# Down product of a mixture of experts with seven half-size products in place of eight

## The chip, the cores and the metric

The kernel runs on one core of one Trainium2 chip. All arithmetic shown here is in 32-bit floating point. The metric is the device time of one execution in microseconds; before the change it is 651.7 us, the median of three runs (650.91 to 652.51).

## The reference, cut to what matters

Two layers are added to the input x of 2048 tokens by 512. The first picks one of four gated feed-forward matrices by token number. The second normalises, chooses 4 of 32 experts per token by a gate, and adds a shared expert:

```
logits = x @ gate_w.T;  topk_w, topk_ids = top_k(softmax(logits), 4)      # weights normalised to 1
gu = einsum('ech,ehf->ecf', buf, w13)          # buf: the tokens of an expert, 512 wide
g, u = split(gu, 2)                            # 256 each
act = silu(g) * u
eo = einsum('eci,eih->ech', act, w2)           # the down product: 256 -> 512
routed.at[token].add(eo * weight)
out = residual + routed + shared
```

What the change touches is the line with w2, the down product of an expert, and the weighting after it.

## The kernel before, in words

The first part of the kernel (to about 270 us) does the first layer, the gate and the shared expert, and scatters the normalised rows into a table in DRAM, one section per expert. The experts are then ordered by how many tokens they have: *rank* 0 is the fullest. The loop over the 32 ranks (L1132) is unrolled and does, per rank r:

- issue the loads for later ranks on SyncE's queue: the rows of rank r+3 (`fetch`), both weight matrices of rank r+5 (`weights`, L882), each as soon as its tile is free;
- turn the rows of rank r+1 on VectorE (a transpose of 128x1024 at L944) and scale them (L950, L954);
- `up_rank` (L1013): 16 products of 128x128 weights by up to 256 tokens, silu on ScalarE, two multiplications on VectorE that make `aT`, the activations with the inner dimension on the partitions;
- `given` and `tokens_of`: the weights and token numbers of the rows;
- `down_rank` (L1033): for each half of 128 tokens two accumulating products 128x128 by 512 columns into one bank of PSUM (`po`), which ScalarE multiplies by the tokens' weights (`weighted`, L987) into a tile `eo`;
- `push` (L992): an indirect DMA on GpSimd's queue that adds the 128 rows to the output in DRAM. Additions of one rank may overlap; those of different ranks follow each other, since they can hit the same rows.

Ranks up to 17 can hold more than 256 tokens. Their surplus goes through six *blocks* that pack the rests of two or four ranks into 128 rows (`up_block`, `turn_block_act`, `down_block` L1069, and one more `push` per rank, `out<-eo_x`). The widths of ranks 26 and up are 240 and 228 tokens, all others 256:

```
LOW = ((26, 240), (29, 228))
```

The tiles that matter: `eo` has four buffers, `po` two banks, the up products three banks and a share of two more, `aT` two buffers, w2 six. The program is written in the order above; the framework places the instructions on each engine's queue by their readiness in its own plan, so that products of rank r+1 can stand between those of rank r, and sets the waits. The hint `behind` fixes the order of two instructions on one engine.

Of the kernel before, what the change touches and what calls it, by code (L numbers as in the profile page):

```python
# [8 lines left out]
F32 = mybir.dt.float32  # L9
# [3 lines left out]
ALU = mybir.AluOpType  # L13
# [4 lines left out]
P = 128  # L18
T = 2048
D = 512  # L20
# [9 lines left out]
CM = 256  # L30
MJ = CM // P
I = 256
IC = I // P
# [3 lines left out]
NB = 4  # L37
# [9 lines left out]
RW = D + 2 * K + 1  # L47
# [12 lines left out]
def tile_xattn_moe(  # L60
# [15 lines left out]
    nc = tc.nc  # L76

    const = ctx.enter_context(tc.tile_pool(name="const", bufs=1))
# [5 lines left out]
    ps_o = ctx.enter_context(tc.tile_pool(name="ps_o", bufs=2, space=PSUM))  # L84
# [6 lines left out]
    ctx_pool = first.enter_context(tc.tile_pool(name="ctx", bufs=1))  # L91
# [19 lines left out]
    shw13 = keep.tile([P, DC, 2 * I], F32, name="shw13")  # L111
    shw2 = keep.tile([P, IC, D], F32, name="shw2")

    none = const.tile([P, NB, RW], F32, name="none")

    def second_inputs(after_):

# [80 lines left out]
    def behind(ins, other, kind=mybir.DependencyClass.NoSync):  # L198

        tc.add_manual_dep(  # L200
            ins.ins,
            other.ins.name,
            mybir.DependencyInfo(kind, mybir.DependencyReason.DATA),
            reason="order",
        )
# [21 lines left out]
    n = EX * NT  # L227
# [73 lines left out]
    xw = ctx_pool.tile([P, XB], F32, name="xw")  # L301
# [502 lines left out]
        return er, er_x, er_i, over_i  # L804


    muls_s, adds_s = [], []

    def glu_up(xT, w13t, name):
# [131 lines left out]
    def turn_parts(z, name, after_=None):  # L941
        n = z.shape[1] * SQ
        xT = late.tile([P, DC, n], F32, tag=f"xT{n}", name=f"xT_{name}", bufs=2)
        ins = nc.vector.transpose(  # L944
            xT.rearrange("p c (r b) -> p r c b", b=SQ), z.rearrange("p r (a c) -> p r c a", c=DC)
        )
        if after_ is not None:
            behind(ins, after_)
        h = 2 if n > P else DC
        ins = nc.vector.tensor_tensor(  # L950
            xT[:, :h, :], xT[:, :h, :], nwq[:, :h].unsqueeze(2).to_broadcast([P, h, n]), ALU.mult
        )
        for c in range(h, DC):
            nc.scalar.mul(xT[:, c, :], xT[:, c, :], nwq[:, c : c + 1])  # L954
        return xT, ins
# [31 lines left out]
    def weighted(po, wt, name, tag, m=P):  # L987
        eo = last.tile([P, D], F32, tag=tag, name=f"eo_{name}", bufs=4 if tag == "eo" else 2)
        nc.scalar.mul(eo[:m, :], po[:m, :], wt[:m, :])  # L989
        return eo  # L990

    def push(eo, dst, group=None):  # L992

        put = nc.gpsimd.indirect_dma_start(  # L994
            out=out,
            out_offset=bass.IndirectOffsetOnAxis(ap=dst, axis=0),
            in_=eo,
            in_offset=None,
            bounds_check=T - 1,
            oob_is_err=False,  # L1000
            compute_op=ALU.add,
        )
        if group is not None:
            if group in adds:
                tc.declare_no_dep(put.ins, group=group, reason="of one expert: other rows")
            tc.add_to_no_dep_group(group, put.ins)
            adds[group] = put

    def width(r):

        return min([CM] + [n for r_, n in LOW if r >= r_])

    def up_rank(xT, w13t, n, name, after_):  # L1013

        pg = ps_m.tile([P, IC, CM], F32, tag="mm", name="pg")
        pu = [
            ps_m.tile([P, CM], F32, tag="mm", name="pu"),
            ps_t.tile([P, CM], F32, tag="tp", name="pu"),
        ]
        for ps, f in [(pg[:, f, :n], f) for f in range(IC)] + [(pu[f][:, :n], IC + f) for f in range(IC)]:  # L1020
            for c in range(DC):
                last_up = nc.tensor.matmul(  # L1022
                    ps, w13t[:, c, f * P : (f + 1) * P], xT[:, c, :n], start=(c == 0), stop=(c == DC - 1)
                )
        s = last.tile([P, IC, CM], F32, tag="silu", name="s", bufs=2)
        nc.scalar.activation(s[:, :, :n], pg[:, :, :n], AF.Silu)  # L1026
        aT = last.tile([P, IC, CM], F32, tag="aTm", name=f"aT_{name}", bufs=2)
        for f in range(IC):
            ins = nc.vector.tensor_tensor(aT[:, f, :n], s[:, f, :n], pu[f][:, :n], ALU.mult)  # L1029
            behind(ins, after_)  # L1030
        return aT, ins, last_up

    def down_rank(aT, w2t, wt, to, n, r):  # L1033
        for j in range(MJ):
            m = min(P, n - j * P)
            po = ps_o.tile([P, D], F32, tag="po", name="po")
            for f in range(IC):
                nc.tensor.matmul(  # L1038
                    po[:m, :], aT[:, f, j * P : j * P + m], w2t[:, f, :], start=(f == 0), stop=(f == IC - 1)
                )  # L1040
            eo = weighted(po, wt[:, j : j + 1], f"{r}_{j}", "eo", m)
            push(eo[:m, :], to[:m, j : j + 1], f"rank{r}")
# [23 lines left out]
        nc.vector.tensor_copy(aT, tp)  # L1066
        return aT

    def down_block(aT, ws):  # L1069
        m = P // len(ws)  # L1070
        po = ps_o.tile([P, D], F32, tag="po", name="po")
        for f in range(IC):
            for i, (_, w2t) in enumerate(ws):
                rr = slice(i * m, (i + 1) * m)
                nc.tensor.matmul(po[rr, :], aT[:, f, rr], w2t[:, f, :], start=(f == 0), stop=(f == IC - 1))
        return po


# [28 lines left out]
    wt = [weights(0), weights(1)]  # L1107
# [6 lines left out]
    last = ctx.enter_context(tc.tile_pool(name="last", bufs=1))  # L1114
# [17 lines left out]
    for r in range(E):  # L1132
        if r + AHEAD < E:
            got[r + AHEAD] = fetch(r + AHEAD)
        if r + AHEAD in before:
            rows_x[r + AHEAD] = block_in(r + AHEAD)
        for q in ahead[r]:
            if q < E:
                wt.append(weights(q))
        if r == E - 1:  # L1140
            need = nc.values_load(over_i[0:1, 0:1], min_val=0, max_val=E)
        if r + 1 < E:
            xT_next, next_ = turn_parts(got[r + 1][0], f"{r + 1}")
        aT, made, last_up = up_rank(xT, wt[r][0], width(r), f"r{r}", next_)
        pend = block_up(r, turned_x, last_up) if r in before else None
        wr = given(got[r][1], er[:, r : r + 1], f"{r}", made)
        to = tokens_of(got[r][1][:, :, RW - D - 1], to_all[:, r, :], made)
        if r + 1 in before:
            turned_x = block_turned(r + 1, rows_x.pop(r + 1), made)
        down_rank(aT, wt[r][1], wr, to, width(r), r)  # L1150
        if pend:
            n, rs_, ws, a, xw, tox = pend
            aTx = turn_block_act(a, f"x{n}")
            eo = weighted(down_block(aTx, ws), xw[:, 0:1], f"x{n}", "eo_x")
            m = P // len(rs_)
            for i, q in enumerate(rs_):
                part[q] = eo[i * m : (i + 1) * m, :], tox[:m, i : i + 1]
        xT = xT_next
        if r in part:
            push(*part[r], f"rank{r}")  # L1160
# [3 lines left out]
    with tc.If(need > 0):  # L1164
# [57 lines left out]
        n = E * C // P  # L1222
# [94 lines left out]
```

## Time and profile before

| | |
|---|---|
| median of 3 runs | 651.7 us |
| the profiled execution's own time | 652.45 us |
| its span, first to last instruction | 650.6 us |
| PE busy | 621.1 us (95%) |
| DVE busy | 285.2 us (44%) |
| ACT busy | 174.7 us (27%) |
| POOL busy | 245.2 us (38%) |
| L1038 down products, 256 records | 116.5 us |
| L1022 up products, 1024 records | 117.7 + 114.0 us |
| L994 additions to the output, 82 | 100.5 + 24.7 us |

PE is the matrix engine, PEld its weight loads, DVE is VectorE, ACT ScalarE, POOL GpSimd, SP SyncE. A name such as `po<-w,aT_r` is the tile written and the tiles read; `x8` counts the records merged into one row. A bracket at the end of a row holds the engine's idle time before it and what ended it; a wait for several things is put down to the one that came last by the profile. Records of one engine can overlap in time, so the distance between starts tells the pace.

### The profile page before, as it was taken

The numbers are of one execution on the slowest core, as the hardware profiler recorded it, in microseconds if no ns is written. First come the engines' busy times: TensorE is split into PE (matmuls) and PEld (weight loads), VectorE is DVE, ScalarE is ACT, GpSimd is POOL, SyncE is SP. The second block draws the span as 40 slices with busy tenths as digits, with TensorE's granted clock in tenths as the row PEclk, the third lists the DMA queues.
The fourth block names the chain that finished last, engine by engine and source line by source line (L and its number), as shares of the span: only waits on it lengthen the run. The fifth ranks groups of instructions, "written<-read, shape, count | busy, mean of one in ns | idle before, by whom it ended". The sixth has DMA issues, their size and how long they took to land.

```text
span 650.6 us, 8462 instructions
## 1 busy us (share of the span) xinstructions
PE 621.1 (95%) x2396; PEld 375.3 (58%) x2396; DVE 285.2 (44%) x766; ACT 174.7 (27%) x311; POOL 245.2 (38%) x217
## 2 busy tenths in 40 slices
PE   5999999999996999999999999999999999999991
PEld 2454555555542444556557577567567777687780
DVE  7655556675733812633424344243243342424410
ACT  1223454454321000122222222222222223222220
POOL 4451002356573465432234333424332413233331
PEclk9999999999996999999999999999999999999997
DMA  7489990325272596799979979979999999998442
GB/s 260 132 316 422 417 418 34 129 88 213 101 268 110 168 398 200 197 313 177 273 170 250 283 146 291 299 162 275 287 270 272 262 245 267 236 260 126 60 51 35
DMA packets 90120, 144.42 MB, mean 222 GB/s; under 512 B 19152, under 2 KB 56016, under 8 KB 83408
## 3 DMA queue, kind: packets, MB, share of 16 engines
q1 hardware_dynamic: 72064, 101.53, 50.5%
q0 software_dynamic: 18000, 42.26, 27.1%
q8 instruction: 21, 0.34, 0.2%
q14 instruction: 35, 0.29, 0.1%
HBM read 79.05 MB, written 66.00 MB: 223 GB/s over the span
## 4 chain that ended last, share of the span: by engine, by line
PE 76%; DMA 7%; SPq 6%; issue 4%; DVE 2%; another core or an unknown queue 1%; POOL 1%; ACT 1%; DVEq 0%; POOLq 0%
PE po L1038 14%; PE pg L1022 14%; PE pu L1022 14%; PE po L461 10%; PE pp L440 9%; SPq L897 4%; PE pg L816 3%; DMA w<-in_w 3%; PE tp L429 2%; PE po L831 2%; PE pp_x L1051 2%; PE pu L816 2%; DMA out<-eo,to_all 2%; DMA z<-s_dram 2%
## 5 line engine op out<-in xcount | busy, mean ns | idle before, releaser
L994 POOL DMA_INDIRECT out<-eo,to_all x64 | 100.5, 1571 | 147.9 <-ACT eo L989 90.2
L1022 PE MATMUL pg<-xT,w 128*128 128x256 f32 (+2 forms) x512 | 117.7, 377 | 0.0
L1038 PE MATMUL po<-w,aT_r 128*128 128x512 f32 (+2 forms) x256 | 116.5, 595 | 0.1
L1022 PE MATMUL pu<-xT,w 128*128 128x256 f32 (+2 forms) x512 | 114.0, 376 | 0.0
L1022 PEld LDWEIGHTS pg<-xT,w 128*128 128x128 f32 x512 | 96.3, 190 | 27.2 <-issue 17.0
L1029 DVE TENSOR_TENSOR aT_r<-s,pu 128x256 f32<-128x256 f32 (+2 forms) x64 | 26.7, 417 | 186.7 <-PE pu L1022 169.7
L1022 PEld LDWEIGHTS pu<-xT,w 128*128 128x128 f32 x512 | 97.3, 190 | 11.5
L989 ACT ACTIVATE eo<-po,wt 128x512 f32<-128x512 f32 x64 | 44.0, 687 | 148.8 <-PE po L1038 147.8
L1038 PEld LDWEIGHTS po<-w,aT_r 128*128 128x128 f32 (+2 forms) x256 | 47.6, 188 | 51.5 <-issue 40.0
L614 POOL DMA_INDIRECT s_dram<-h,slot x64 | 62.2, 973 | 36.0 <-issue 16.3
L440 PE MATMUL pp<-cT,xT 128*128 (+1 forms) x152 | 72.1, 597 | 1.4 <-issue 0.6
L461 PE MATMUL po<-cT,aT 128*128 (+1 forms) x152 | 68.4, 592 | 0.0
L944 DVE STREAM_TRANSPOSE xT<-z 128x1024 f32<-128x1024 f32 x32 | 65.2, 2038 | 3.2 <-DMA z<-s_dram 2.8
L994 POOL DMA_INDIRECT out<-eo_x,to_x x18 | 24.7, 1371 | 89.9 <-DMA out<-eo,to_all 43.2
L461 PEld LDWEIGHTS po<-cT,aT 128*128 128x128 f32 x152 | 27.5, 190 | 27.7 <-issue 27.5
L440 PEld LDWEIGHTS pp<-cT,xT 128*128 128x128 f32 x152 | 26.7, 190 | 27.4 <-issue 24.3
L583 POOL TENSOR_TENSOR rs<-rs,mhalf 128x2 f32<-128x2 f32 x16 | 11.3, 704 | 78.8 <-DVE rs L582 78.8
L1026 ACT ACTIVATE s<-pg 128x512 f32<-128x512 f32 (+2 forms) x32 | 18.9, 590 | 71.2 <-PE pg L1022 65.1
L954 ACT ACTIVATE xT<-xT,nwq 128x256 f32<-128x256 f32 x64 | 28.7, 498 | 23.7 <-DVE xT L944 10.2
L831 PE MATMUL po<-shw,aT_s 128*128 128x512 f32 x64 | 32.5, 650 | 2.1 <-issue 1.8
L816 PE MATMUL pg<-h2T,shw 128*128 128x512 f32 x64 | 29.2, 596 | 0.0
L403 ACT ACTIVATE hn<-acc,rv 128x512 f32 (+1 forms) x19 | 15.2, 802 | 50.8 <-DVE rv L387 30.9
(186 smaller groups left out, 541.7 us busy)
## 6 DMA issues: line engine op xcount, KB each, us to landing
w<-in_w SPq DMA_DIRECT2D x32, 1024.0 KB
s_dram<-none SPq DMA_DIRECT2D x1, 20840.0 KB
w<-in_w SPq DMA_DIRECT2D x32, 512.0 KB
z<-s_dram SPq DMA_DIRECT2D x128, 128.0 KB
h_dram<-h SPq DMA_DIRECT2D x4, 1042.0 KB
cT<-in_ctxT SPq DMA_DIRECT2D x4, 1024.0 KB
out<-none SPq DMA_DIRECT2D x1, 1024.0 KB
s_dram<-h,slot POOLq DMA_INDIRECT x64
```

Of the source, the lines that this page charges most:

```text
L440: ins = nc.tensor.matmul(ups[b], xT_[b][:, c, :], cT[:, bass.ds(off[b], 1), c, :].rearrange("p o f -> p (o f)"), start=(c == 0), stop=(c = ...
L461: ins = nc.tensor.matmul(po, aT_[b][:, f, :], cT[:, bass.ds(off[b], 1), f, :].rearrange("p o f -> p (o f)"), start=(f == 0), stop=(f == DC ...
L614: put = nc.gpsimd.indirect_dma_start(out=table, out_offset=bass.IndirectOffsetOnAxis(ap=index, axis=0), in_=src, in_offset=None,)
L816: ins = nc.tensor.matmul(ps, w13t[:, c, fo * P : (fo + 1) * P], xT[:, c, :], start=(c == 0), stop=(c == DC - 1))
L831: ins = nc.tensor.matmul(po, aT[:, f, i * P : (i + 1) * P], w2t[:, f, :], start=(f == 0), stop=(f == IC - 1))
L944: ins = nc.vector.transpose(xT.rearrange("p c (r b) -> p r c b", b=SQ), z.rearrange("p r (a c) -> p r c a", c=DC))
L954: nc.scalar.mul(xT[:, c, :], xT[:, c, :], nwq[:, c : c + 1])
L989: nc.scalar.mul(eo[:m, :], po[:m, :], wt[:m, :])
L994: put = nc.gpsimd.indirect_dma_start(out=out, out_offset=bass.IndirectOffsetOnAxis(ap=dst, axis=0), in_=eo, in_offset=None, bounds_check=T ...
L1022: last_up = nc.tensor.matmul(ps, w13t[:, c, f * P : (f + 1) * P], xT[:, c, :n], start=(c == 0), stop=(c == DC - 1))
L1029: ins = nc.vector.tensor_tensor(aT[:, f, :n], s[:, f, :n], pu[f][:, :n], ALU.mult)
L1038: nc.tensor.matmul(po[:m, :], aT[:, f, j * P : j * P + m], w2t[:, f, :], start=(f == 0), stop=(f == IC - 1))
```

## The change

Ranks with the full width of 256 (0 to 25) take another down product. The activations (256 tokens by 256) and the weights (256 by 512) are each seen as 2x2 blocks, 128x128 and 128x256. Strassen's scheme (in Winograd's form) makes the four blocks of the result from seven block products. VectorE makes the sums: four of weight blocks (`w2_sums`, tiles t1 to t4, ahead of the up products) and four of activation blocks (s1, s2, s4, and one in place in `aT`). The products accumulate in two `po` banks: products 1, 6, 7 and 4 in one half of the first (`u`), product 2 in its other half, 5 and 3 in the second. Between the products the partial results are read out with the tokens' weights: four times by ScalarE (`put`) and three times by VectorE, which adds to what is in `eo` (`add`). The two `eo` tiles of a rank are both in work at once. `down_block` keeps its products behind the rank's last product by a new argument. The tile `none`, a source of blank rows, moves to a pool that is given up after the first layer.

```
-    none = const.tile([P, NB, RW], F32, name="none")
+    none = ctx_pool.tile([P, NB, RW], F32, name="none")
...
+    HD = D // 2
...
+    def w2_sums(w2t, r):
+
+        (b11, b12), (b21, b22) = [[w2t[:, f, j * HD : (j + 1) * HD] for j in range(2)] for f in range(IC)]
+        t1, t2, t3, t4 = [last.tile([P, HD], F32, tag=f"t{i}", name=f"t{i}_r{r}") for i in range(1, 5)]
+        for dst_, x_, y_ in ((t1, b12, b11), (t2, b22, t1), (t3, b22, b12), (t4, b21, t2)):
+            nc.vector.tensor_tensor(dst_, x_, y_, ALU.subtract)
+        return {1: b11, 2: b21, 3: b22, 4: t4, 5: t1, 6: t2, 7: t3}
+
+    def down_rank_by_halves(aT, R, wt, to, r):
+
+        (a11, a12), (a21, a22) = [[aT[:, f, i * P : (i + 1) * P] for f in range(IC)] for i in range(2)]
+        s1, s2, s4 = [last.tile([P, P], F32, tag=f"s{i}", name=f"s{i}_r{r}") for i in (1, 2, 4)]
+        nc.vector.tensor_tensor(s1, a21, a22, ALU.add)
+        nc.vector.tensor_tensor(s2, s1, a11, ALU.subtract)
+        nc.vector.tensor_tensor(s4, a12, s2, ALU.subtract)
+        nc.vector.tensor_tensor(a21, a11, a21, ALU.subtract)
+        L = {1: a11, 2: a12, 3: s4, 4: a22, 5: s1, 6: s2, 7: a21}
+        p12 = ps_o.tile([P, 2, HD], F32, tag="po", name="po")
+        p5 = ps_o.tile([P, HD], F32, tag="po", name="po")
+        eo = [last.tile([P, 2, HD], F32, tag="eo", name=f"eo_{r}_{j}", bufs=4) for j in range(2)]
+
+        def product(ps, i, first_):
+            return nc.tensor.matmul(ps, L[i], R[i], start=first_, stop=True, skip_group_check=True)
+
+        def put(i, j, ps):
+            nc.scalar.mul(eo[i][:, j, :], ps, wt[:, i : i + 1])
+
+        def add(i, j, ps):
+            nc.vector.scalar_tensor_tensor(eo[i][:, j, :], ps, wt[:, i : i + 1], eo[i][:, j, :], ALU.mult, ALU.add)
+
+        u = p12[:, 0, :]
+        product(u, 1, True)
+        put(0, 0, u)
+        product(p12[:, 1, :], 2, False)
+        add(0, 0, p12[:, 1, :])
+        product(p5, 5, True)
+        put(1, 1, p5)
+        product(u, 6, False)
+        put(0, 1, u)
+        product(p5, 3, False)
+        add(0, 1, p5)
+        push(eo[0].rearrange("p j d -> p (j d)"), to[:, 0:1], f"rank{r}")
+        product(u, 7, False)
+        add(1, 1, u)
+        ins = product(u, 4, False)
+        put(1, 0, u)
+        push(eo[1].rearrange("p j d -> p (j d)"), to[:, 1:2], f"rank{r}")
+        return ins
...
-    def down_block(aT, ws):
+    def down_block(aT, ws, after_=None):
...
-                nc.tensor.matmul(po[rr, :], aT[:, f, rr], w2t[:, f, :], start=(f == 0), stop=(f == IC - 1))
+                ins = nc.tensor.matmul(po[rr, :], aT[:, f, rr], w2t[:, f, :], start=(f == 0), stop=(f == IC - 1))
+                if after_ is not None:
+                    behind(ins, after_)
+                after_ = ins
...
+        R = w2_sums(wt[r][1], r) if width(r) == CM else None
         aT, made, last_up = up_rank(xT, wt[r][0], width(r), f"r{r}", next_)
...
-        down_rank(aT, wt[r][1], wr, to, width(r), r)
+        if R is not None:
+            last_up = down_rank_by_halves(aT, R, wr, to, r)
+        else:
+            down_rank(aT, wt[r][1], wr, to, width(r), r)
...
-            eo = weighted(down_block(aTx, ws), xw[:, 0:1], f"x{n}", "eo_x")
+            eo = weighted(down_block(aTx, ws, last_up), xw[:, 0:1], f"x{n}", "eo_x")
```

## The prediction

> **What bounds the kernel now.** I read the core's own line first (650.6 us, granted clock 0.985), then the stretches of the rank stage, then TensorE's instructions in order of time, then the queue that adds the results to the output.
>
> The stretches, columns: time, length, then busy us and instructions of PE, PEld, DVE, ACT and POOL, granted clock, DMA share, GB/s.
>
> ```profile
> 450.00:470.00 20.00, 20.00 (x109) 12.14 (x108) 5.27 (x10) 5.22 (x10) 6.58 (x5) 1.00 1.13 285
> ...
> 510.00:530.00 20.00, 20.00 (x78) 14.61 (x77) 7.79 (x14) 5.37 (x10) 5.70 (x5) 1.00 1.00 260
> ```
>
> TensorE is never idle between 330 and 630 us, at the full clock. VectorE is busy 39% and ScalarE 27% in the steady stretch. The DMA engines' packets fill their time as well (0.99 as the mean of the fourteen such stretches from 310 to 590 us), so a second resource stands close behind TensorE.
>
> TensorE in order of time, one steady rank:
>
> ```profile
> 534.15 3.60 PE L1038 MATMUL po<-w,aT_r 128*128 128x512 f32 x8
> 537.58 3.19 PE L1022 MATMUL pg<-xT,w 128*128 128x256 f32 x14
> 540.60 3.62 PE L1022 MATMUL pu<-xT,w 128*128 128x256 f32 x16
> 544.06 0.59 PE L1022 MATMUL pg<-xT,w 128*128 128x256 f32 x2
> 544.49 3.60 PE L1038 MATMUL po<-w,aT_r 128*128 128x512 f32 x8
> ```
>
> Starts give the pace, not the durations, which overlap. A rank takes 544.49 - 534.15 = 10.34 us. Every product stands as two records: the four down products are 8 records in 537.58 - 534.15 = 3.43 us, 0.429 each; the 16 up products are 32 records, 0.216 each (540.60 to 544.06, 16 of them). The two pg records at 544.06 belong to the next rank: TensorE's order already puts other work into a wait for VectorE. Another such place, in a block:
>
> ```profile
> 415.53 0.38 PE L1064 MATMUL tp_x<-ident,a_x 128*128 128x128 f32 x2
> ...
> 415.75 1.03 PE L1022 MATMUL pg<-xT,w 128*128 128x256 f32 x4
> ...
> 415.95 0.43 DVE L1066 COPY aT_x<-tp_x 128x256 f32<-128x256 f32 x1 [2.12 <-PE tp_x L1064]
> ...
> 416.70 1.92 PE L1075 MATMUL po<-w,aT_x 128*32 128x512 f32 x16
> ```
>
> This is a full hop TensorE, VectorE, TensorE: from the end of issue (415.75, the next start) the copy ends 0.63 later and the next product starts after 0.95. Two up products, 4 x 0.216 = 0.86 us, cover nearly all of it.
>
> The queue of additions to the output, and the end of the chain of waits:
>
> ```profile
> 578.59 1.64 POOL L994 DMA_INDIRECT out<-eo,to_all  x1 [6.85 <-ACT eo L989]
> 580.53 1.55 POOL L994 DMA_INDIRECT out<-eo,to_all  x1 [0.30 <-issue]
> 588.84 1.55 POOL L994 DMA_INDIRECT out<-eo,to_all  x1 [6.75 <-DMA out<-eo,to_all]
> ...
> 636.68 1.61 POOL L994 DMA_INDIRECT out<-eo,to_all  x1 [4.41 <-ACT eo L989]
> ```
>
> ```profile
> 621.97 6.03 DMA out<-eo,to_all
> ...
> 630.68 5.21 DMA out<-eo,to_all
> ```
>
> Counting pairs back from the last (rank 31 at 636.68), 588.84 is rank 25. Its products start at 575.48 and its first result is weighted 2.66 us later (534.15 to 536.12 + 0.69 in the steady rank), at 578.1. So its addition starts 10.7 us after its result. The wait at 578.59 names ScalarE, but that rank's own result was long done; what fits is the landing before, about 8.3 us after each second addition (580.53 to 588.84). Ranks add one after the other, and this chain runs a whole rank behind TensorE, with room for two ranks (four eo tiles). In the last six ranks, when the loads are over, it catches up to within 0.4 us. So two chains end together: TensorE, and the landings.
>
> **The change, part by part.**
>
> *TensorE.* Out: 26 x 8 records at 0.429. In: 26 x 14 records of width 256; the up products have that shape, at 0.216. Per rank 3.43 - 3.02 = 0.41 us, over 26 ranks 10.6 us. The weight load takes 190 ns (L1022 PEld), inside the pace of 216, as in the up products.
>
> *The serial chain.* Products 1, 6, 7 and 4 share one half of a bank, product 2 the other half, 3 and 5 another bank; between them ScalarE or VectorE reads. The trace shows no two results in one bank. The Trainium skill's PSUM — Partial Sum Buffer, "PSUM bank collisions raise a hardware error", asks that reads and TensorE's writes be kept apart by bank, not by address. By it product 2 waits for the read of 1, and 6 for that of 2: four hops in series (1 to 2, 2 to 6, 6 to 7, 7 to 4). A hop without cover costs some 0.9 us by the copy above; products 5 and 3 fill 0.43 each of two. That leaves 4 x 0.9 - 0.86 = 2.7 us per rank for other work; by address alone it would be two hops less half, 1.4 us. I take 2.7. The cover is the next rank's up products: 6.9 us per rank, and the two examples show that they are put there. Full cover costs nothing; none costs 2.7 - 0.41 = 2.3 us per rank, 60 us in all. The balance tips at 0.41 us uncovered. I take 0.1 (the 0.95 against 0.86 of the copy's hop, once per rank): 2.6 us.
>
> *VectorE.* 128x256 from L1029: 0.42 us. 128x128, not in the trace: L1029 also has 228 columns at 392 ns, so about 1.04 ns a column and 0.29 us. New per rank: four weight sums 1.68, four activation sums 1.15, three additions 1.26, together 4.1 us. It has 4.1 now (transpose 2.04, scaling 0.69, two multiplications 0.84, three small ones 0.55). 8.2 of 9.9 us: not the bound, but a sum can find a transpose of 2.04 us in front of it in the queue; then product 7 or 4 is late, and behind it everything in TensorE's order. The weight sums lie beside the up products, at nothing; uncovered they cost 1.7 per rank.
>
> A rule against these sums: the Trainium skill's SBUF — State Buffer, "Who interferes with whom", says that a VectorE instruction with two SBUF inputs contends with a GpSimd instruction that reads SBUF, and the later one blocks in full. The row: L950, also two SBUF inputs, takes 676/693/694 ns (least, median, most) in all 32 ranks, one at 505.73 inside an addition's 505.06 to 506.39. By the rule one sum per rank could stand up to 1.55 us, 40 us of VectorE time in 26 ranks; by the row none. I take the row.
>
> *ScalarE.* Two of 687 ns become four of about 383 (L1056, 128x256 out of PSUM): 0.16 us more per rank, on an engine that is 73% idle.
>
> *Moved in time.* The number of additions and their bytes stay. But eo[0] is complete only after products 1, 2, 5, 6 and 3 with their reads: by the hops above some 4.4 us after the first product, where it was 2.66: 1.7 later. And both eo tiles are first written earlier, so a tile has to be free about 1.5 us sooner. That makes the landings' room smaller. The second weights are freed after product 4, some 2 us later, five ranks ahead of need: nothing. *none* in another pool: its transfers end before the ranks start; nothing, and if not, the first rank's tiles wait once.
>
> *Landings.* From rank 10 (417.09, the last addition that follows its result within 2.5 us) to the end of the loads, additions follow landings, not TensorE. Up to there TensorE's gain is 10 x 0.41 = 4.1, less 1.7 for the later result: 2.4 us. Of the remaining 16 x 0.41 = 6.5 us the landings pass on something between nothing (the engines' share is 0.99) and all (stretches with share 1.13 and 285 GB/s show room). I take a fifth, since rank 14 to 25 hardly show a gap: 1.3 us. Sum 3.7 us. TensorE alone, 10.6 - 2.6 = 8.0, would allow more; the later chain decides. 650.6 - 3.7 = 646.9 of span; 1.85 us lie around it in the profiled execution (652.45), and the median of 651.7 lies 0.75 below that. 651.7 - 3.7 = **648.0 us**.
>
> **The rivals.**
>
> *All of the gain.* The landings move with the loads, which TensorE releases, and speed up with it. For: rank after rank the landings keep TensorE's 10.34 exactly. Against: share 0.99, and the lag grew from 2.4 us at rank 10 to 11 at rank 18. 651.7 - 8.0 to 10.6: 641 to 644.
>
> *No gain.* The earlier claim on eo and the later eo[0] eat what the first ten ranks bring: 650 to 653.
>
> *Slower.* The place: the addition on VectorE that frees product 4. If a 2.04 us transpose is queued before it and TensorE's order has too little in that hole, TensorE stands. From 0.41 us per rank it decides, that is one rank in five hit in full. With 0.9 us per rank, 26 x (0.9 - 0.41) = 13: 664. For: VectorE 83% taken (8.2 of 9.9), seven reads of PSUM per rank where there were two, each one more link between queues whose planned length can be off. Against: both examples of filling in the trace, and 6.9 us to fill with.
>
> *The change does not do what it says*: a 256-wide record slower than half a 512-wide one. 0.216 against 0.2145: excluded by the up products.
>
> **How the numbers follow.** A part of the gain 0.44 (own range 645.5 to 650), all 0.10, none 0.16, slower 0.30 (653 to 672, middle near 661). The range 642 to 663 leaves out about half of "all" and the upper 0.12 of "slower". 0.3% is 2 us, about what a measurement of this kernel can tell from no change: faster means below 649.75. That is 0.10 and most of the first case: 0.50; within 0.19; slower 0.31.
>
> **What would show it.** Seven products as 14 records at 0.216 in 26 ranks; a steady rank's period at 9.9 (full), near 10.2 (landings) or above 10.34 (slower); pg and pu records between the products; idle of PE with VectorE or ScalarE named as releaser (slower), or ScalarE waiting for a DMA before it writes eo (landings). VectorE near 8 us per rank. L950 and the sums stretched beyond 0.7 and 0.42 would bring the port rule back. The prediction is wrong if TensorE shows holes over 0.41 us per rank, or if the additions stop running a rank late.

## The result, and the profile after

The changed kernel takes 659.0 us (median of 4 runs, 658.2 to 661.2) where the kernel before takes 651.7 beside it: 1.0103 times the time before, with an interval of 1.0070 to 1.0136. The forecast was 648.0. The profiled execution took 658.2 us with a span of 656.4, so 5.8 us more of span. One thing must be known to read the numbers below: some kernels here spread by up to 22 us from run to run, and a ratio with its interval leaves out the runs that lie over 1.5% above the fastest of their kernel, so the median and the range of all runs stand beside it where the two tell different things. From series to series the kernel before stood at 643 to 652 us, so each variant is compared with the runs of the kernel before in its own series.

The same stretches as before the change, in the changed kernel (time, length, busy us and records of PE, PEld, DVE, ACT and POOL, granted clock, DMA share, GB/s):

```profile
450.00:470.00 20.00, 19.38 (x112) 12.34 (x111) 11.70 (x26) 5.26 (x11) 8.24 (x6) 1.00 1.12 273
...
490.00:510.00 20.00, 17.01 (x68) 13.36 (x68) 10.77 (x30) 4.82 (x10) 7.74 (x6) 0.91 1.07 281
510.00:530.00 20.00, 18.02 (x82) 14.80 (x82) 13.88 (x34) 6.33 (x13) 4.43 (x4) 1.00 0.90 225
530.00:550.00 20.00, 18.91 (x88) 15.77 (x87) 14.07 (x33) 5.85 (x12) 5.99 (x4) 1.00 0.99 261
```

TensorE, which had no idle time from 330 to 630 us, now stands (at the full granted clock but for the first of the three, 0.91) for 3.0, 2.0 and 1.1 us of three stretches in a row (20.00 less the first busy column), and for 7.2 us in 490 to 590 together. Before that point the change does what it says. TensorE in order of time, one plain rank of the changed kernel:

```profile
375.22 0.59 PE L1056 MATMUL po<-w,aT_r 128*128 128x256 f32 x2
375.65 1.03 PE L1023 MATMUL pg<-xT,w 128*128 128x256 f32 x4
376.51 0.59 PE L1056 MATMUL po<-t_r,s_r 128*128 128x256 f32 x2
...
381.78 3.62 PE L1023 MATMUL pu<-xT,w 128*128 128x256 f32 x16
385.24 0.59 PE L1056 MATMUL po<-w,aT_r 128*128 128x256 f32 x2
```

The rank takes 385.24 - 375.22 = 10.02 us where it took 10.34. Between the seven products stand 14 `pg` records of the next rank, 3.0 us of cover. So at TensorE the saving is real: 0.32 us per plain rank. It is lost later. Of the waits of the changed kernel from 270 to 640 us, those in which ScalarE's writing of `eo` waits for an addition's landing, and TensorE's products for that writing (us in total, times, longest):

```profile
PEld po L1056 <- ACT eo L1059: 15.3, 29, 2.4
...
ACT eo L1059 <- DMA out<-eo,to_all: 14.2, 8, 2.6
...
PE po L1056 <- ACT eo L1059: 7.1, 8, 2.0
```

ScalarE waits for a landing before it can write an `eo` tile, and TensorE waits for ScalarE, because its next product goes where the last result still stands unread (product 3 into the bank of product 5). In the profile of the kernel before, ScalarE never waits for the landing of an addition. The chain that ended last, a piece of it (start, us, what):

```profile
529.78 0.39 POOL out L995
530.17 1.47 issue
531.64 9.15 DMA out<-eo,to_all
...
540.88 0.48 ACT eo L1059
541.36 0.04 issue
541.40 1.13 PE po L1056 x4
```

The second addition of rank 19 is issued at 531.64 and lands at 540.79. At that moment ScalarE gets the tile, and 0.6 us later TensorE goes on. DMA has 15% of the whole chain (7% before), of which landings of `out<-eo` are 10%, and TensorE 66% (76% before).

The largest hole, in rank 18, shows the same path, and then a second cost. First ScalarE and TensorE in order of time, then two stretches of 2 us:

```profile
505.36 0.47 ACT L1059 ACTIVATE eo<-po,wt 128x256 f32<-128x256 f32 x1 [2.64 <-DMA out<-eo,to_all]
...
505.89 1.12 PE L1056 MATMUL po<-w,s_r 128*128 128x256 f32 x2 [1.99 <-ACT eo L1059]
```

```profile
506.00:508.00 2.00, 2.00 (x5) 1.64 (x6) 0.10 (x1) 0.10 (x1) 1.62 (x2) 0.51 1.18 179
508.00:510.00 2.00, 2.00 (x7) 1.60 (x6) 0.81 (x2) 0.37 (x1) 1.70 (x2) 0.64 1.02 377
```

Right behind this hole the granted clock is 0.51 and 0.64. The eight records from 505.89 to 509.36 take 3.47 us, where the plain pace of 0.216 us makes 1.73: some 1.7 us are lost that no idle time shows. In the run with seven products in ranks 18 to 25 alone (e7, below) the clock falls to 0.50 and 0.69 behind the first holes; behind the next longest hole of the changed kernel, 1.65 us at 518.4, it stays at 1.00. What decides is not shown.

Why the landing is now too late is seen in ScalarE's writes. Kernel before, the two writes of rank 20, and between them the first addition of rank 19:

```profile
525.77 0.69 ACT L989 ACTIVATE eo<-po,wt 128x512 f32<-128x512 f32 x1 [4.20 <-PE po L1038]
...
527.19 1.55 POOL L994 DMA_INDIRECT out<-eo,to_all  x1 [6.91 <-ACT eo L989]
...
527.49 0.69 ACT L989 ACTIVATE eo<-po,wt 128x512 f32<-128x512 f32 x1 [1.03 <-PE po L1038]
```

Changed kernel, rank 20's first two of four writes, and then rank 21's:

```profile
528.64 0.47 ACT L1059 ACTIVATE eo<-po,wt 128x256 f32<-128x256 f32 x1 [1.50 <-DVE wt L974]
529.38 0.47 ACT L1059 ACTIVATE eo<-po,wt 128x256 f32<-128x256 f32 x1 [0.27 <-PE po L1056]
...
538.66 0.47 ACT L1059 ACTIVATE eo<-po,wt 128x256 f32<-128x256 f32 x1 [1.49 <-DVE wt L974]
540.88 0.47 ACT L1059 ACTIVATE eo<-po,wt 128x256 f32<-128x256 f32 x1 [1.74 <-DMA out<-eo,to_all]
```

Before, a rank's second tile is written 1.72 us after its first. Now it would be 0.74 us after (528.64 to 529.38). With four tiles, the second tile of rank r is the second tile of rank r-2, and free when that rank has landed. In the kernel before, the profile does not show when rank 18 landed: the bracket at 527.19 names ScalarE, whose result had long been done. By an estimate it was at about 526.4: the addition of rank 19 starts at 527.19, and from a landing to the next addition it is 0.78 us (540.79 to 541.57 in the changed kernel; 0.79 in the prediction's lines, 630.68 + 5.21 to 636.68). The write of rank 20 came at 527.49. So the kernel before had about 1.1 us of room at this place, and the change claims the tile 1.0 us earlier after the first, besides TensorE's being ahead.

The time by ranks, from the start of each rank's `pu` products:

| rank's start | before | changed | difference |
|---|---|---|---|
| 0 | 276.47 | 275.39 | -1.08 |
| 10 | 404.44 | 401.82 | -2.62 |
| 18 | 499.24 | 496.49 | -2.75 |
| 19 | 509.58 | 511.56 | +1.98 |
| 20 | 519.92 | 524.00 | +4.08 |
| 26 | 581.75 | 587.29 | +5.54 |
| 31 | 630.52 | 636.05 | +5.53 |

Up to rank 18 TensorE gains 2.75 - 1.08 = 1.7 us (the rank stage began 1.1 us earlier in this execution, in work that the change does not touch). Ranks 18 to 25 then take 90.8 us where they took 82.5; that is 10.6 more than eight plain ranks of 10.02; the holes of 7.2 us and the 1.7 us at the low clock are most of that. From rank 26 on, with the old down product and the loads over, the distance stays.

### The profile page after: what moved, and what is told of

The parts are those of the page before. It is cut to its first block, busy times and chain, and to the rows that moved or that the text cites. A ratio compares the mean times of both kernels' runs of the same rounds, so it can differ in the third digit from the quotient of the medians.

```text
span 656.4 us, 9220 instructions
## 1 busy us (share of the span) xinstructions
PE 618.2 (94%) x2552; PEld 397.8 (61%) x2552; DVE 378.8 (58%) x1052; ACT 190.0 (29%) x363; POOL 246.2 (38%) x217
## 4 chain that ended last, share of the span: by engine, by line
PE 66%; DMA 15%; DVE 6%; issue 4%; SPq 3%; POOL 2%; another core or an unknown queue 1%; ACT 1%; POOLq 0%; DVEq 0%; ACTq 0%
DMA out<-eo,to_all 10%; PE pg L1023 10%; PE pu L1023 10%; PE po L461 9%; PE pp L440 9%; PE po L1056 7%; PE po L1088 3%; PE pp_x L1101 3%; PE pg L817 3%; PE pu L817 3%; PE tp L429 2%; PE po L832 2%; SPq L898 2%; DMA z<-s_dram 2%; DVE xT L945 1%
## 5 line engine op out<-in xcount | busy, mean ns | idle before, releaser
L995 POOL DMA_INDIRECT out<-eo,to_all x64 | 101.2, 1582 | 157.2 <-DVE eo L1062 63.1
L1023 PE MATMUL pg<-xT,w 128*128 128x256 f32 (+2 forms) x512 | 134.1, 379 | 0.0
L1059 ACT ACTIVATE eo<-po,wt 128x256 f32<-128x256 f32 x104 | 49.2, 473 | 153.9 <-PE po L1056 102.8
L1062 DVE SCALAR_TENSOR_TENSOR eo<-po,wt,eo 128x256 f32<-128x256 f32 x78 | 37.6, 483 | 16.5 <-PE po L1056 10.9
L1039 DVE TENSOR_TENSOR t_r<-w,t_r 128x256 f32<-128x256 f32 x52 | 21.8, 418 | 34.9 <-PE po L1056 34.4
L583 POOL TENSOR_TENSOR rs<-rs,mhalf 128x2 f32<-128x2 f32 x16 | 11.3, 704 | 77.9 <-DVE rs L582 77.9
L1056 PE MATMUL po<-w,aT_r 128*128 128x256 f32 x104 | 33.2, 401 | 1.3 <-ACT eo L1059 1.3
L1056 PE MATMUL po<-t_r,s_r 128*128 128x256 f32 x104 | 32.1, 390 | 0.6 <-DVE eo L1062 0.2
L1056 PE MATMUL po<-t_r,aT_r 128*128 128x256 f32 x104 | 31.1, 381 | 0.1
```

Of the source, the lines that this page charges most:

```text
L995: put = nc.gpsimd.indirect_dma_start(out=out, out_offset=bass.IndirectOffsetOnAxis(ap=dst, axis=0), in_=eo, in_offset=None, bounds_check=T ...
L1023: last_up = nc.tensor.matmul(ps, w13t[:, c, f * P : (f + 1) * P], xT[:, c, :n], start=(c == 0), stop=(c == DC - 1))
L1056: return nc.tensor.matmul(ps, L[i], R[i], start=first_, stop=True, skip_group_check=True)
L1059: nc.scalar.mul(eo[i][:, j, :], ps, wt[:, i : i + 1])
L1062: nc.vector.scalar_tensor_tensor(eo[i][:, j, :], ps, wt[:, i : i + 1], eo[i][:, j, :], ALU.mult, ALU.add)
```

## The experiments

Three theories. *Landings*: the additions, one rank after another, are the bound, and the change takes buffer room from them. *The saving itself is at fault or not there*: order of the products, hops without cover. *VectorE*: its 4 us of new sums and additions per rank delay what feeds TensorE, or GpSimd's issuing. The expectations of e1 to e4 are in us and were set for a kernel before at 651.7; in their series it took 643.3, so they are read here by their distance to it.

**The chain of additions opened.** The additions of rank r go to one of four outputs, three of which nothing reads, in the changed kernel (e4) and in the kernel before (e5). An addition then waits for the landing of four ranks before:

```
+    out_more = [dram.tile([T + PAD, D], F32, name=f"out_{i}") for i in range(3)]
...
+        k = int(group[4:]) % 4 if group is not None else 0
         put = nc.gpsimd.indirect_dma_start(
-            out=out,
+            out=out if k == 0 else out_more[k - 1],
```

> The changed kernel with the additions of rank r sent to one of four outputs, so that an addition follows that of four ranks before and not the last; same number, same bytes, but three quarters of the routed part lands in outputs that nothing reads. A: the loop is open, TensorE's own gain remains less its small holes, 643 to 648 us. B: full DMA engines hold it up all the same, 652 to 660. C: 655 or more.

> The kernel before, with the additions of rank r going to one of four outputs, so that a rank waits for the landing four ranks back; three quarters of the routed part land in outputs that nothing reads. With it, the changed kernel ran in 0.990 of the time before. Landing theory: the kernel before is bound by TensorE as soon as the chain is open, at 0.998 to 1.002 (its TensorE has no holes to lose), and the whole difference of about 1% to the changed kernel with four outputs is Strassen's saving, some 5 to 7 us of the 10.6. If opening the chain was itself the gain and Strassen gives nothing: 0.990 here too.

Measured: the changed kernel 0.9902 (0.9873 to 0.9932), the kernel before 0.9961 (0.9935 to 0.9986). Both stop spreading: 11 runs of the first lie within 1.4 us, 12 of the second within 2.3. The changed kernel so opened, the same stretches, and then GpSimd's queue in order of time:

```profile
490.00:510.00 20.00, 20.00 (x94) 16.85 (x93) 15.16 (x37) 6.79 (x14) 6.16 (x5) 1.00 1.10 280
510.00:530.00 20.00, 20.00 (x94) 16.85 (x93) 15.16 (x37) 6.80 (x14) 6.16 (x5) 1.00 1.08 292
```

```profile
526.67 1.55 POOL L997 DMA_INDIRECT out<-eo,to_all  x1 [6.40 <-DVE eo L1064]
528.74 1.55 POOL L997 DMA_INDIRECT out<-eo,to_all  x1 [0.52 <-ACT eo L1061]
536.69 1.55 POOL L997 DMA_INDIRECT out<-eo,to_all  x1 [6.40 <-DVE eo L1064]
```

Holes gone, the additions follow their results every 10.02 us, and the DMA engines carry the same bytes at that pace (share 1.10 and 1.08). The order of the instructions on TensorE, VectorE and ScalarE is that of the changed kernel, and so is VectorE's load of 15 of 20 us. So neither of these is what costs, and the DMA engines' capacity is not either. Nor do the other outputs make an addition faster: from issue to landing it takes 7.3, 8.3 and 10.2 us (least, median, most; 490 to 570 us), as long as the 7.0 to 9.8 of the second additions of the changed kernel on the chain that ended last. What costs is the wait of one rank's additions for the rank before. With that wait loosened a loss of 1.0% is a gain of 1.0%, of which 0.4% come to the kernel before as well, where at most 0.2% was expected, and 0.6%, some 4 us, are Strassen's, where 5 to 7 us were.

**TensorE's saving alone.** In the kernel before, one of the four down products of each rank is half as wide in ranks 0 to 25. This leaves out the second half of the inner sum for 128 tokens by 256 columns, 0.43 us per rank at TensorE, and moves nothing else:

```
+                c = D // 2 if n == CM and j == MJ - 1 and f == IC - 1 else D
...
-                    po[:m, :], aT[:, f, j * P : j * P + m], w2t[:, f, :], start=(f == 0), stop=(f == IC - 1)
+                    po[:m, :c], aT[:, f, j * P : j * P + m], w2t[:, f, :c], start=(f == 0), stop=(f == IC - 1),
...
```

> The kernel before with one of its four down products at half width in ranks 0 to 25: the same 0.43 us less of TensorE per rank, 11 us in all, without sums, hops or earlier claims on eo. It leaves out the second half of the inner sum for 128 tokens and 256 columns. If TensorE alone sets the end: 640 to 642 us. If the landings set it (A and B): the gain is passed on only where additions still follow their results, 646 to 651.

Measured: 1.0022 (0.9990 to 1.0054), median 648.0 of 20 runs (641.3 to 658.1) beside 643.3. Eleven us less work for TensorE, and no gain, not even the part that the landing theory left. In its profile, of a run longer than the median, ScalarE waits for landings 21 times, though its writes are those of the kernel before (waits view: us in total, times, longest):

```profile
ACT eo L989 <- DMA out<-eo,to_all: 90.2, 21, 10.1
```

**Where the loss arises.** Seven products in ranks 18 to 25 alone (e7), or in ranks 0 to 13 alone (e6):

```
-        R = w2_sums(wt[r][1], r) if width(r) == CM else None
+        R = w2_sums(wt[r][1], r) if 18 <= r < 26 else None
```

> Seven products in ranks 18 to 25 alone. Landing theory: ranks 0 to 17 are those of the kernel before, so the additions reach rank 18 about 11 us behind their results as before; the earlier claim on the eo tiles then meets them at once: ScalarE waits for landings in ranks 18 to 25, TensorE gains nothing, 1.000 to 1.010. If a gain of TensorE's were passed on even in part: 8 x 0.3 us, 0.996 to 0.998.

> Seven products in ranks 0 to 13 alone; ranks 14 to 25 take the down product of before. Landing theory: TensorE's lead from the early ranks (about 2 to 4 us) runs into the full eo tiles in ranks 14 to 25, as it did when TensorE's saving was tried alone: 0.998 to 1.003. The loss of the full change comes from the tiles' earlier claim in the late ranks and is gone here. If the loss came from anything in the early ranks (VectorE's sums, their order): as much as half of it stays, 1.005 or more.

Measured: e7 1.0109 (1.0079 to 1.0138), beside 1.0100 (1.0038 to 1.0163) for the changed kernel run again. The eight late ranks alone cost as much as the whole change, just above what was expected, and the wait is the one expected. ScalarE's writes in e7 that wait for a landing first, in order of time:

```profile
505.77 0.47 ACT L1059 ACTIVATE eo<-po,wt 128x256 f32<-128x256 f32 x1 [4.65 <-DMA out<-eo,to_all]
507.37 0.47 ACT L1059 ACTIVATE eo<-po,wt 128x256 f32<-128x256 f32 x1 [1.12 <-DMA out<-eo,to_all]
```

e6 did not go as expected: 1.0038 (0.9971 to 1.0105) rests on three of its 12 runs, and the median is 665.1 (650.8 to 671.6), 13 us over the 652.0 of the kernel before. So the late ranks suffice for the loss, but the early ones are not harmless; the run with the chain open, below, tells how they act.

> The changed kernel once more, beside the variants, because two runs of the kernel before differed by 8 us between chips. Landing theory (the additions to the output, one rank after another, are the bound, and the change takes buffer room from them): again 1.005 to 1.014 times the kernel before, and slower than its own variant with eight eo tiles, which stood at 1.000. If the order of the work or VectorE's load is what costs: the same ratio, so this run alone does not tell; it is the reference for the next three.

**The tiles' room.** Eight `eo` tiles in place of four: in the changed kernel twice (e1), in the kernel before (e2), and in e7 (e15); and three tiles in the kernel before (e16). To make room for eight, the rarely entered last part of the kernel gets one buffer fewer of a tile of its own.

```
-        eo = [last.tile([P, 2, HD], F32, tag="eo", name=f"eo_{r}_{j}", bufs=4) for j in range(2)]
+        eo = [last.tile([P, 2, HD], F32, tag="eo", name=f"eo_{r}_{j}", bufs=8) for j in range(2)]
```

> The changed kernel with eight eo tiles in place of four; every engine's order in the rank stage stays. Theory A (closed loop: ScalarE waits for a landed addition before it may write eo, TensorE waits for ScalarE, the next loads wait for TensorE, and the landing waits behind the loads): ScalarE no longer waits for a landing, the 8 us of holes on TensorE between 490 and 590 us go, and the time falls to 649 to 653 us. Theory B (the DMA engines are full, the landings take what they take, and room only moves the wait): 656 to 661 us, with the end set by additions that run further behind. Theory C (the new sums on VectorE slow the additions at their shared port): the landings stay late by 6 us whatever the tiles, 657 to 661.

> The changed kernel with eight eo tiles, once more: at 1.0004 it left the landings free of the tiles' room but its times spread from 640 to 660 us. If the room alone is the cost: 0.990 to 0.995 here, like the kernel with four outputs. If the landings themselves are slower when TensorE runs ahead: 1.000 or more again, with additions every 11 us or more in ranks 18 to 25.

> The kernel before with eight eo tiles, and with none in the pool of the first layer, which makes room for them. Nothing waits for eo before, so A, B and C all expect 650.5 to 653 us; it also shows what the move of none costs alone, which I take to be nothing.

> Seven products in ranks 18 to 25 alone, which cost the whole 1.0109, with eight eo tiles in place of four. If the loss of these ranks is the tiles' claim (ScalarE waiting for a landing two ranks back): 0.996 to 1.001, no ScalarE wait on a landing and no hole of TensorE behind ScalarE in 490 to 590 us. If the loss is slower landings in themselves: 1.005 or more, with additions every 10.6 us as before and the lag growing through the eight tiles.

> The kernel before with three eo tiles in place of four, nothing else moved. Landing theory: in ranks 18 to 25 the landing of rank r-2 comes some 0.4 us before rank r writes its tile, so the kernel before stands at the edge of the same wait; with a tile less, ScalarE waits for landings and TensorE gets holes: 1.005 to 1.02, as in the changed kernel. If there is room left: 0.998 to 1.002.

| kernel | tiles | ratio | interval | median, range (us) | before in its series |
|---|---|---|---|---|---|
| changed | 4 | 1.0100 | 1.0038 to 1.0163 | 658.7, 656.4 to 665.6 | 652.0 |
| changed | 8 | 1.0004 | 0.9964 to 1.0045 | 651.4, 639.8 to 660.4 | 643.3 |
| changed | 8 | 0.9982 | 0.9939 to 1.0025 | 657.7, 649.2 to 664.4 | 652.2 |
| before | 8 | 1.0018 | 0.9986 to 1.0050 | 644.1, 643.0 to 654.3 | 643.3 |
| seven products in 18 to 25 | 4 | 1.0109 | 1.0079 to 1.0138 | 659.1, 658.0 to 660.8 | 652.2 |
| seven products in 18 to 25 | 8 | 1.0009 | 0.9961 to 1.0057 | 649.7, 641.3 to 652.9 | 643.6 |
| before | 3 | 1.0039 | 0.9997 to 1.0080 | 649.1, 641.7 to 658.1 | 643.6 |

By the ratio, four more tiles take away the whole loss of the change and of its late ranks, and they do nothing for the kernel before. By the medians they take away little: 8.1 and 5.5 us over the kernel before for the changed kernel, where it was 6.7, and 6.0 for e15, where e7 had 6.9. The runs tell why. With four tiles every run of the changed kernel and of e7 is 4 us or more over the median of the kernel before; with eight it is 16 of 22, 6 of 12 and 7 of 12, and the rest lie within 4 us of it or below. In the profile of the second e1, one of its short runs (649.25), ScalarE waits for no landing, and TensorE has no holes (windows):

```profile
490.00:510.00 20.00, 20.00 (x93) 16.86 (x92) 15.17 (x37) 6.69 (x15) 7.73 (x5) 1.00 1.03 261
510.00:530.00 20.00, 20.00 (x93) 16.84 (x93) 15.16 (x37) 6.72 (x15) 7.15 (x6) 1.00 1.05 259
```

The profile of e15 is of a longer run (650.2). There ScalarE waits for no landing either, and TensorE has no holes from 490 to 610 us. But TensorE no longer ends the kernel. The last rank's first result, and its first addition:

```profile
623.95 0.69 ACT L990 ACTIVATE eo<-po,wt 128x512 f32<-128x512 f32 x1 [4.19 <-PE po L1088]
...
635.41 1.60 POOL L995 DMA_INDIRECT out<-eo,to_all  x1 [4.92 <-DMA out<-eo,to_all]
```

The result is done at 624.64, and its addition starts 10.8 us later, behind a landing. In the kernel before it was 0.4 us, in the second e1 2.4. The profile of the first e1, its longest run (660.4), has 16.4 us there, and even with eight tiles ScalarE waits for landings four times (11.3 us), with a hole of 4.5 us in TensorE from 550 to 570. So the tiles' room ends the waits of ScalarE in the shorter runs, and in the longer ones moves them to the end of the kernel, where the additions come late by themselves. This is what the expectation of the first e1 called theory B; only its reason, that full DMA engines set the pace, does not fit e4. No version with one output beat the kernel before by more than its interval.

Three tiles in the kernel before: the ratio's interval touches no change, but nine of the 12 runs are 4 us or more over the kernel before's median (7 of 36 of that kernel), and even in a short run (641.95) ScalarE waits for landings five times, 14.7 us in all. So this kernel too stands near the edge, with a room of about 1.1 us, not the 0.4 that the expectation had.

**VectorE's sums alone.** The kernel before, with the eight sums per rank added and read by nothing (e8); the same with the chain open (e14); and the early ranks, e6, with the chain open (e17):

```
+        if width(r) == CM:
+            w2_sums(wt[r][1], r)
         aT, made, last_up = up_rank(xT, wt[r][0], width(r), f"r{r}", next_)
...
+        if width(r) == CM:
+            sums_alone(aT, r)
         down_rank(aT, wt[r][1], wr, to, width(r), r)
```

> The kernel before with only the eight sums of VectorE per rank added in ranks 0 to 25, written to tiles that nothing reads; products, additions and their tiles are as before. Landing theory: VectorE is not in the chain, 0.998 to 1.003. If VectorE's load is what costs (a transpose or a sum in front of the multiplications that feed TensorE, or contention with GpSimd's issuing of the additions): 1.006 or more, with the issue of an addition longer than its 1.57 us or holes of TensorE behind VectorE.

> The kernel before with VectorE's eight sums per rank added and read by nothing, and with the additions of rank r going to one of four outputs (three quarters of the routed part land in outputs that nothing reads). With one output the sums made half of the runs 6 to 22 us longer though no product moved. If the sums act only through the chain of additions (they shift the loads, and the landings fall among them otherwise): with the chain open the times are those of the kernel before with four outputs, 0.994 to 0.998, and do not spread. If VectorE's load delays TensorE or the loads by itself: 1.003 or more, with a spread.

> Seven products in ranks 0 to 13 alone, with the additions going to four outputs (three quarters of the routed part land in outputs that nothing reads). With one output most of its runs were 9 to 20 us longer. If that came from the chain of additions: 0.992 to 0.996 here (the kernel before with four outputs, less about half of Strassen's saving at TensorE), without a spread. If early ranks lose by VectorE's queue: 0.998 or more.

Measured: e8 1.0013 (0.9966 to 1.0059), but a median of 665.0 of 13 runs (651.6 to 674.1) beside 652.0: eight of the 13 are 6 to 22 us longer. e14 0.9960 (0.9931 to 0.9989), 12 runs within 1.4 us: the same as the kernel before with the chain open (0.9961). e17 0.9951 (0.9919 to 0.9983): its median of 640.9 lies 1.5 us under that of e14, and the range is 640.6 to 647.5 where e6 went from 650.8 to 671.6. So the sums and the early ranks cost nothing by themselves: VectorE's load costs time only where the chain of additions is closed. That it acts by shifting what the landings meet fits this, but is not shown. The profiled run of e8, a long one, shows what it then looks like, in a kernel whose products and additions are those of before (waits view):

```profile
POOL out L994 <- DMA out<-eo,to_all: 136.8, 19, 10.3
...
ACT eo L989 <- DMA out<-eo,to_all: 75.7, 19, 7.4
```

**Fewer loads in the late ranks.** Ranks 18 to 25 use rank 17's weights, and 1.5 MB per rank are not loaded, in the changed kernel (e9) and in the kernel before (e10):

```
-                wt.append(weights(q))
+                wt.append(wt[17] if 18 <= q < 26 else weights(q))
```

> The changed kernel with the weights of ranks 18 to 25 left out of the loads: these ranks use rank 17's. Landing theory: loads and additions share the DMA engines; in ranks 26 to 31, after the loads, an addition of a rank follows the one before after 7.8 us, and with loads after 10.3 to 10.6. Without these loads (1.5 MB per rank) ranks 18 to 25 should add every 10.0 us or less, TensorE's own pace, ScalarE should not wait for landings, TensorE's 7 us of holes close: 0.985 to 0.992 of the kernel before. If an accumulating addition takes its 10 us by itself, or the holes come from VectorE: no change, 1.005 or more.

> The same loads left out of the kernel before. Landing theory: TensorE is the bound here and had no holes, so little is won: 0.995 to 1.000, as with four outputs (0.996); the additions stop running a rank late. The distance to the changed kernel with the same cut is then Strassen's saving at TensorE, 4 to 6 us. If loads bound the kernel before by themselves: below 0.99.

Measured: e10 0.9998 (0.9980 to 1.0017), as expected: its additions no longer run a rank late (rank 18's first at 505.7 where it was at 516.9) and TensorE sets the time. e9 1.0053 (1.0030 to 1.0077), a miss. Landings hold up nothing there either: no ScalarE wait on a landing, additions with their results. But TensorE has a new hole in each of these ranks: with the weights at hand, the framework's plan puts the instructions in another order. TensorE in one rank of e9, then VectorE at the same place:

```profile
515.25 1.03 PE L1023 MATMUL pg<-xT,w 128*128 128x256 f32 x4
516.78 0.67 PE L1056 MATMUL po<-w,s_r 128*128 128x256 f32 x2 [0.51 <-DVE s_r L1048]
```

```profile
513.75 0.28 DVE L1046 TENSOR_TENSOR s_r<-aT_r 128x128 f32<-128x128 f32 x1
513.95 0.15 DVE L974 TENSOR_REDUCE wt<-ws 128x2 f32<-128x8 f32 x1
514.02 2.04 DVE L945 STREAM_TRANSPOSE xT<-z 128x1024 f32<-128x1024 f32 x1
515.96 0.28 DVE L1047 TENSOR_TENSOR s_r<-s_r,aT_r 128x128 f32<-128x128 f32 x1
```

The transpose of 2.04 us stands between the first and the second activation sum; the third sum then keeps TensorE idle for 0.5 to 0.8 us when the cover has run out, and a rank takes 10.76 us (506.02 to 516.78) where the changed kernel takes 10.02. In the changed kernel the transpose comes after all four sums of activations. So e9 does not tell what fewer loads do for the changed kernel; it shows the mechanism of the prediction's slower rival, at work in another kernel.

## Why the prediction was wrong, point by point

**TensorE's saving: right in a rank, too high in the sum.** 0.31 us per rank net was forecast, 0.32 was measured in plain ranks (10.34 to 10.02). The total is 4.5 us and not 8.0: with the chain open, from the start of rank 0 to that of rank 31, e4 takes 349.6 us and e14 354.1. In three of the block ranks (5, 10 and 14) 0.7 to 0.9 us are given back each time; why is not settled.

**The serial chain and its cover: right.** 2.7 us of other work between the products was taken, by reading a bank as one thing; 3.0 us stand there. The transpose in front of a sum, the rival with 0.30, did not decide here: VectorE takes 7.4 of a plain rank's 10.02 us, not 8.2, and its order was a good one. e9 shows that with another order it costs 0.74 us per rank, near the 0.9 of the forecast.

**The port rule: the row was right to be taken.** The Trainium skill's SBUF — State Buffer, "Who interferes with whom", taken as the prediction took it, would have let a sum stand for an addition's whole issue. L951, the scaling that was L950, takes 673 to 708 ns in the ranks with a median of 693 as before, the weight sums 405 to 450 or 370 to 427, and the additions' issue 1582 ns on average after 1571.

**Landings and "moved in time": the step that failed.** The sum took two things from this term: 2.4 us that the additions of the first ten ranks would bring, and "a fifth, since rank 14 to 25 hardly show a gap: 1.3 us". Neither came. The additions of rank 10 start 0.8 us earlier (416.3 after 417.1), less than the 1.1 us by which the rank stage began earlier. And late ranks pass on nothing: the saving alone stands at 1.0022. The larger error is one of pricing. The prediction saw that "a tile has to be free about 1.5 us sooner" and that this "makes the landings' room smaller", but put no wait on it. The room was about 1.1 us, and could have been read from the trace of before: write of the second tile against the next rank's addition less its 0.8 us. What the runs showed in place of the nothing that the sum had here: with four tiles the wait costs 7.2 us of holes on TensorE and 1.7 us at a low clock, and all runs of the changed kernel and of e7 are 4 us or more longer; with eight tiles a quarter to a half of the runs are not. In the others the chain of additions itself ends late. The sum let that chain pass on a fifth of the late ranks' gain, and it passed on none; opened, it turns 1.010 into 0.990. A wait for a landing, with ScalarE between it and TensorE, was named as what to look for; it had no case with a chance of its own among the slower ones.

**The rivals.** "No gain" named the right place, the earlier claim on `eo`, and stopped at zero. What turned it into a loss is that the claimed tile is not only late for an addition: ScalarE, standing at it, leaves a half bank unread, and the serial chain of seven products has no way round it. One late landing stops TensorE; that the next results and loads, which TensorE releases, then come later too and feed the delay is argued, not shown. The range of 642 to 663 holds the 659.0 only because of the slower case, and that case had another mechanism, a transpose on VectorE: that is luck.

**What stays open.** What makes one landing take 7.0 us after its issue (522.04 to 529.00) and the next 9.2 (531.64 to 540.79), and why the runs of a kernel at this edge differ by 20 us, is not settled. Without loads it is faster: in the kernel before rank 26 follows rank 25 by 7.7 us (588.84 to 596.58), after 10.3 between the ranks ahead of it. That the landings fall otherwise among the loads when anything is shifted fits e3, e6 and e8, but no run shows it directly. How the loss divides between the tiles' room and the late additions can't be told either, since with eight tiles one run has the first cost gone and another the second grown.

## What to carry to other kernels

Before work is taken off the busiest engine, look for a chain that only just keeps its pace: here accumulating DMAs that wait for one another ran a whole rank late, and the margin, about 1.1 us, was to be read as the time between a buffer's becoming free and its next write. A change that writes a buffer earlier, or holds two where it held one, spends that margin, and has to be priced as a wait with all that stands behind it. If the chain can be opened as a trial, that run tells in one step whether the saving is real: here it turned 1.010 into 0.990. More buffers alone are a weaker trial: here they let the additions fall further behind, and most of the longer runs stayed.

## What was not expected of the hardware

- ScalarE's weighting of 128x256 out of PSUM takes 473 ns, not half of the 687 ns of 128x512 and not the 383 of a plain activation of that width; VectorE's weighted addition of 128x256 takes 484 where 420 was taken. The seven reads of a rank are 4 x 473 + 3 x 484 = 3.3 us, the two of before were 1.4.
- Kernels held up by waiting accumulations can spread by 22 us between runs (e8), and the same instructions without that wait by 1.4 (e14). It is not always so: e7, held up the same way, stays within 2.8.
- Behind TensorE's largest hole the granted clock was 0.51 and 0.64 for some 4 us, and the records that otherwise take 0.216 us took 0.43 on average.
- The DMA engines do not need the 10.3 us per rank: with the chain open they carry the same bytes every 10.02, at a share of 1.10.
